# The start of a two-layer attention kernel: a block of its own for the first normalisation, and the sums of three weight matrices divided and queued anew

## The chip, the cores and the metric

The kernel runs on one core of a Trainium2 chip. The metric is the device time of one execution in microseconds (us), as the median of several runs; lower is better. Besides, one execution was taken by the hardware profiler, and all times of single instructions come from that one. The core has five engines that run side by side, each through its own list of instructions in order, and wait for each other through semaphores: TensorE (PE in the profile) multiplies matrices, VectorE (DVE) and ScalarE (ACT) work on tiles, GpSimd (POOL) works on tiles and issues transfers, SyncE (SP) issues transfers only.

## The reference

The input is a batch of 8 images of 32 x 32 positions with 512 channels, in float32. Two layers follow each other; each adds the result of an attention over the group-normalised input to the input:

```
x = x + conv0(_gn(x))     # softmax(q k^T * 32**-0.5) v, 16 heads of 32, then w_proj and b_proj
x = x + conv1(_gn(x))     # 4 heads of 128, with relative position logits from pos_emb_w and pos_emb_h, then Wo
_gn(v): mean and variance over the positions and the 16 channels of each of 32 groups, eps 1e-5
```

Here q, k and v are products of the normalised input (1024 positions x 512 channels per batch) with 512 x 512 weights, all in float32.

## The kernel before

**Tiles and stages.** One batch is a block of 128 partitions x 4 chunks x 1024 positions: the channels lie on the partitions, so x is kept transposed. There are eight such blocks of memory in one pool (`block`, line 75); they are handed out anew as soon as the last use of an old one is over, and then the first write of the new one waits for it. A loop over the batches weaves together the first attention of batch b, the second layer of batch b − 1 and the loading and first projections of batch b + 1.

**Seven products.** Each 512 x 512 projection is done with seven products of half-size matrices instead of eight. For that, each weight matrix needs four differences of its quarters (`add_up`, line 138), and each input four sums and differences of its quarters, the forms (`forming`, line 332; f_xn in the profile). `seven` (line 390) runs the products in the order 0, 5, 1, 4, 6, 2, 3 into three banks x, y and z, and copies or adds the results between them: p1 and p7 are copies by ScalarE (L399, L418), a and b are sums by VectorE (L404, L412), and the four quarters of the result are written by ScalarE (L475), VectorE (L478, L481) and GpSimd (L485). In the profile these banks carry the name of what is projected: x_v, y_v, z_v for v, and so on. The second product into y of a unit (number 4) starts over in y when a has been read out of it, and the third (number 2) when b has been.

**What stands at the start.** `load_first` (line 802) loads the first batch's rows (x_rows) through the queues of SP and ScalarE, then v's weights through SP. TensorE transposes the rows, ScalarE copies the result to x0T (L827), TensorE does six matmuls that nobody reads (L831), and VectorE gathers statistics (L251, L252). `put_away` (line 216) then writes x0T to DRAM through SP's queue (d in the profile), because it is added again after the attention; `group_norm` (line 257) makes mean and variance by some ten small operations on VectorE (L277 to L288), the reciprocal root on GpSimd (L292, rstd), and normalises x0T in place in four quarters (L296). The forms follow. GpSimd makes v's differences meanwhile (L147) and stores them to DRAM (L149). q's and k's weights are loaded by SP after that, and all eight of their differences are made by VectorE behind the last form (`issue_after(last_form[0].ins)`, which is an order, not a wait). Then `before_first` (line 838) runs the first unit of v, of q and of k, and the loop begins.

The second batch is fetched by `load` (line 780): pieces of x (xs, four transfers of 64 KB for each) through SP's queue into three buffers, transposed by VectorE (L794). A scheduler places the instructions of each engine in an order of its own; `issue_after` binds it. A transfer of SP also waits until one issued eight transfers earlier has landed.

Of the kernel before, what the change touches and what calls it, by code (L numbers as in the profile page):

```python
# [13 lines left out]
ALU = mybir.AluOpType  # L14
# [13 lines left out]
def quick_path(  # L28
# [23 lines left out]
    nc = tc.nc  # L52
# [22 lines left out]
    def block(name, shape=None, dtype=F32):  # L75
        return mem.tile(shape or [P, CC, N], dtype, tag="block", name=name, bufs=BLOCKS)

    def chunks(block):
        return [block[:, i, :] for i in range(CC)]
# [36 lines left out]
    check_at = [0]  # L116


    HC, HN = CC // 2, NB // 2

    def quarter(w, i):
# [3 lines left out]
    class Matrix:  # L125
# [9 lines left out]
            whole = t[:, : CC // 2, :].rearrange("p a (b n) -> p (a b) n", n=NB)  # L135
            queue.dma_start(whole, self.w)

        def add_up(self, engine, store, keep=False):

            t = self.t  # L140
            whole = t[:, : CC // 2, :].rearrange("p a (b n) -> p (a b) n", n=NB)
            sums = t[:, CC // 2 :, :].rearrange("p a (b c n) -> p (a b) c n", c=HC, n=HN)
            b11, b12, b21, b22 = [quarter(whole, i) for i in (11, 12, 21, 22)]
            for i, (x, y) in enumerate(
                [(b12, b11), (b22, sums[:, 0]), (b22, b12), (b21, sums[:, 1])]
            ):
                engine.tensor_tensor(sums[:, i], x, y, op=ALU.subtract)  # L147
            d = dram.tile([P, 4, HC, HN], F32, tag="sums", name=f"ws_{self.name}", bufs=8)
            store.dma_start(d, sums)  # L149
            self.t = d  # L150
            self.kept = (whole, sums) if keep else None
# [17 lines left out]
    class Stream:  # L169
# [41 lines left out]
        def ahead(self):  # L211
            use = next(self.uses, None)
            if use is not None:
                self.load(*use)

    def put_away(xT, name):
        kept = []
        for cc in range(CC):
            d = dram.tile([P, N], F32, tag="kept", name=f"d_{name}_{cc}", bufs=4 * CC)
            nc.sync.dma_start(d, xT[cc])  # L220
            kept.append(d)
        return kept

# [10 lines left out]
    def load_blocks(b, cc, h):  # L234

        xs = mem.tile([P, NB // 32, 32], F32, tag="row", name=f"xs_{b}_{cc}_{h}", bufs=3)
        for a in range(P // 32):
            nc.sync.dma_start(
                xs[32 * a : 32 * a + 32],
                by_blocks(xf[b, h * NB : (h + 1) * NB, :], cc * P + 32 * a),  # L240
            )
        return xs.rearrange("p t i -> p (t i)")
# [11 lines left out]
            s.rearrange("p h s -> p (h s)"),  # L254
        )

    def group_norm(st, xT, name, after=None, behind=None):

        mv = st.pop("mv")

        def averages(out, src, tag):
            total = small.tile([P, 2], F32, tag=f"total{tag}", name=f"total{tag}_{name}")
            nc.vector.tensor_reduce(
                total, src.rearrange("p (g k) -> p g k", k=GROUP_CHANNELS), axis=AX.X, op=ALU.add
            )
            nc.vector.tensor_scalar(
                out.rearrange("p (g k) -> p g k", k=GROUP_CHANNELS),
                total.unsqueeze(2).to_broadcast([P, 2, GROUP_CHANNELS]),
                1.0 / GROUP_CHANNELS,
                None,  # L270
                op0=ALU.mult,
            )

        turned = small.tile([P, 32], F32, tag="turned", name=f"turned_{name}")

        with tc.issue_after(after().ins) if after is not None else nullcontext():
            nc.vector.transpose(turned, mv)  # L277
        avg = small.tile([P, 2, 32], F32, tag="avg", name=f"avg_{name}")
        averages(avg[:, 0, :], turned, 0)

        nc.vector.tensor_sub(turned, turned, avg[:, 0, :])
        nc.vector.tensor_mul(turned, turned, turned)
        averages(avg[:, 1, :], turned, 1)
        back = small.tile([P, 2, 32], F32, tag="back", name=f"back_{name}")
        nc.vector.transpose(back.rearrange("p a c -> p (a c)"), avg.rearrange("p a c -> p (a c)"))
        mean = back[:, 0, :CC]
        var = small.tile([P, CC], F32, tag="var", name=f"var_{name}")
        nc.vector.scalar_tensor_tensor(  # L288
            var, back[:, 0, CC : 2 * CC], GN_EPS, back[:, 1, :CC], op0=ALU.add, op1=ALU.add
        )  # L290
        rstd = small.tile([P, CC], F32, tag="rstd", name=f"rstd_{name}")
        nc.gpsimd.tensor_tensor(rstd, var, neg_half, op=ALU.pow)  # L292
        yield 0
        for cc in range(CC):
            with tc.issue_after(behind().ins) if behind is not None else nullcontext():
                nc.vector.tensor_scalar(  # L296
                    xT[cc],
                    xT[cc],
                    mean[:, cc : cc + 1],
                    rstd[:, cc : cc + 1],  # L300
                    op0=ALU.subtract,
                    op1=ALU.mult,
                )
            if cc % 2:
                yield 0
# [3 lines left out]

    begun = [None]  # L310
    half_done = [None]
    last_form = [None]

    added = [None]

# [41 lines left out]
    def forms(x, name, room=None):  # L357
        got = []

        def whole():  # L360
            got.append((yield from forming(x, name, room)))

        run(whole())
        return got[0]
# [415 lines left out]
    def load(b, st):  # L780

        x = xT = None
        parts = [(cc, h) for cc in range(CC) for h in range(NH)]
        ahead = [load_blocks(b, *parts[i]) for i in range(2)]
        for i, (cc, h) in enumerate(parts):
            xs = ahead.pop(0)
            if i + 2 < len(parts):
                ahead.append(load_blocks(b, *parts[i + 2]))
            if h == 0:
                yield 0  # L790
            if x is None:
                x = block(f"x0T_{b}")
                xT = chunks(x)
            nc.vector.transpose(xT[cc][:, h * NB : (h + 1) * NB], xs)  # L794
            if h == NH - 1:
                statistics(st, xT, cc, f"0_{b}")
        yield 0
        st["kept"] = put_away(xT, f"0_{b}")
        yield from group_norm(st, xT, f"0_{b}")
        st["xn"] = yield from forming(x, f"xn0_{b}", behind=lambda: added[0])  # L800

    def load_first(st):

        rows = block("x_rows", [P, NT, C])
        for t in range(NT):
            queue = nc.scalar if t % 2 else nc.sync
            queue.dma_start(rows[:, t, :], xf[0, t * P : (t + 1) * P, :])
        WV0.fetch(nc.sync)
        x = block("x0T_0")
        xT = chunks(x)  # L810
        for h in range(NH):
            if h == 0:
                whole = psum.tile([P, CC, NB], F32, tag="ps", name="turned_0", bufs=1)
                banks = [whole[:, cc, :] for cc in range(CC)]
            else:
                banks = [bank(f"turned_1_{cc}") for cc in range(CC - 1)]
                banks.append(psum.tile([P, NB], F32, tag="acc", name="turned_1", bufs=1))
            for t in range(NT // NH):
                for cc in range(CC):
                    nc.tensor.transpose(  # L820
                        banks[cc][:, t * P : (t + 1) * P],
                        rows[:, h * (NT // NH) + t, cc * P : (cc + 1) * P],
                        ident,
                    )
            for cc in (0, 2, 1, 3):
                part = xT[cc][:, h * NB : (h + 1) * NB]
                nc.scalar.copy(part, banks[cc])  # L827

        idle = psum.tile([P, CC, NB], F32, tag="ps", name="idle", bufs=1)
        for t in range(6):  # L830
            nc.tensor.matmul(idle[:, t % CC, :], ident, rows[:, t, :], start=True, stop=True)  # L831
        for cc in (0, 2, 1, 3):
            statistics(st, xT, cc, "0_0")
        st["kept"] = put_away(xT, "0_0")
        run(group_norm(st, xT, "0_0"))
        st["xn"] = forms(x, "xn0_0")

    def before_first(st):

# [139 lines left out]
    def run(part):  # L979
        for _ in part:  # L980
            pass
# [34 lines left out]
    WQ0, WK0, WV0 = [Matrix(w_qkv, i * C, f"qkv{i}") for i in range(3)]  # L1016
# [19 lines left out]

    states = [{} for _ in range(B)]
    load_first(states[0])
    WV0.add_up(nc.gpsimd, nc.gpsimd, keep=True)
    for m in (WQ0, WK0):  # L1040
        m.fetch(nc.sync)

        with tc.issue_after(last_form[0].ins):
            m.add_up(nc.vector, nc.gpsimd, keep=True)
    fill_sel()
    stream = Stream(plan)

    def other_sums():
        for m in (WP, WQ1, WK1, WV1, WO):
            m.fetch(nc.gpsimd)  # L1050
            m.add_up(nc.gpsimd, nc.gpsimd)
            yield 0

    def at_once(do):
# [1 line left out]
        return  # L1056
        yield

    run(before_first(states[0]))
    for b in range(B + 1):  # L1060
        rest, total = [], 0
        s = [None] * 2 + states + [None] * 2
# [547 lines left out]
```

## Time and profile before

| | us |
|---|---|
| median of 3 runs (lowest, highest) | 3852.97 (3852.47, 3856.44) |
| profiled execution | 3854.03 |
| its span, first to last instruction | 3852.2 |
| mean granted TensorE clock | 0.997 |
| TensorE busy | 3793.3 |
| VectorE busy | 2555.5 |
| TensorE's wait ahead of the first v product | 5.4 |

Busy time is the time in which an engine had an instruction under way. A row of the order of time gives start, length, engine, line, operation and tiles, the count of equal instructions that were merged, and in brackets the idle time before it with what ended it. Matmuls overlap, so a row's length is a little more than its share of the engine. The granted clock is TensorE's, as a share of full speed.

### The profile page before, as it was taken

What the parts mean: (1) busy time and instruction counts of PE and PEld (TensorE: products, weight loads), DVE (VectorE), ACT (ScalarE), POOL (GpSimd) and SP (SyncE); (2) the same over time, 40 slices, a digit from 0 to 9 for tenths busy, and PEclk for the clock granted to TensorE, in tenths of its full rate; (3) what the DMA queues carried; (4) which work ended last, traced back from release to release, by engine and by line L of the source; (5) the groups of instructions that cost most, each with busy time, mean ns of one, the idle gap of its engine ahead of it and who ended that gap; (6) DMA issues with size and microseconds to landing.
All of it is one profiled execution on the core that took longest, in us unless ns stands there. A gap on an engine that the chain in (4) does not pass through costs nothing. (4 is left out here: it accounts for less than half of the span.)

```text
span 3852.2 us, 79876 instructions
## 1 busy us (share of the span) xinstructions
PE 3793.3 (98%) x34478; PEld 1376.7 (36%) x34478; DVE 2555.5 (66%) x2964; ACT 1760.4 (46%) x1830; POOL 620.8 (16%) x400
## 2 busy tenths in 40 slices
PE   8999999999999999999999999999999999999998
PEld 4222244232443224432344323433234332334353
DVE  6777675676755867568665686656866568665545
ACT  2554554545444454444544445444454445553132
POOL 2341101121101210112100121111210112001201
PEclk9999999999999999999999999999999999999999
DMA  6122120143202322023220231203411033110321
GB/s 184 60 87 79 42 60 3 37 126 65 59 6 73 98 57 56 12 89 85 49 55 16 93 91 37 52 20 96 91 39 43 24 97 77 31 39 31 105 45 26
DMA packets 482983, 234.72 MB, mean 61 GB/s; under 512 B 269600, under 2 KB 461376, under 8 KB 481600
## 3 DMA queue, kind: packets, MB, share of 16 engines
q1 hardware_dynamic: 470992, 213.74, 20.6%
q0 software_dynamic: 2608, 13.70, 1.0%
q8 instruction: 273, 4.47, 0.5%
q10 hardware_dynamic: 9024, 2.10, 0.3%
q14 instruction: 86, 0.70, 0.1%
HBM read 170.72 MB, written 58.72 MB: 60 GB/s over the span
## 5 line engine op out<-in xcount | busy, mean ns | idle before, releaser
L604 ACT ACTIVATE e<-ps 128x2048 f32<-128x2048 f32 x512 | 961.7, 1878 | 839.6 <-PE ps L596 633.5
L626 DVE TENSOR_TENSOR es<-es,e 128x2048 f32<-128x2048 f32 x384 | 893.3, 2326 | 405.9 <-ACT e L604 403.0
L596 PE MATMUL ps<-q,k 32*64 32x512 f32 x8192 | 578.3, 613 | 18.7 <-ACT e L604 18.7
L615 PE MATMUL acc<-e,v 128*32 128x512 f32 x4096 | 547.4, 606 | 0.0
L714 ACT ACTIVATE e<-ps 128x512 f32<-128x512 f32 x512 | 305.7, 597 | 506.9 <-PE ps L712 437.4
L711 PE MATMUL ps<-q,k 128*128 128x512 f32 x1024 | 525.0, 594 | 0.3 <-DVE posT L697 0.3
L723 PE MATMUL acc<-e,v 128*128 128x512 f32 x1024 | 522.0, 593 | 0.3 <-ACT e L714 0.3
L581 POOL TENSOR_TENSOR q<-q,su 128x512 f32<-128x512 f32 x128 | 210.4, 1644 | 1548.9 <-DVE su L577 1428.6
L734 DVE TENSOR_TENSOR es<-es,e 128x512 f32<-128x512 f32 x384 | 291.5, 759 | 249.8 <-ACT e L714 247.2
L712 PE MATMUL ps<-posT,sel 128*128 128x512 f32 x512 | 406.6, 794 | 0.0
L711 PEld LDWEIGHTS ps<-q,k 128*128 128x128 f32 x1024 | 192.5, 190 | 230.2 <-issue 218.5
L596 PEld LDWEIGHTS ps<-q,k 32*64 32x64 f32 x8192 | 120.5, 129 | 411.7 <-issue 221.7
L723 PEld LDWEIGHTS acc<-e,v 128*128 128x128 f32 x1024 | 193.1, 189 | 147.3 <-issue 92.8
L615 PEld LDWEIGHTS acc<-e,v 128*32 128x32 f32 x4096 | 81.3, 108 | 411.9 <-issue 363.8
L624 DVE TENSOR_TENSOR es<-e,e 128x2048 f32<-128x2048 f32 x64 | 173.0, 2704 | 32.4 <-ACT e L604 32.4
L561 DVE STREAM_TRANSPOSE tu<-su 128x512 f32<-128x512 f32 x128 | 90.5, 707 | 97.0 <-ACT su L559 95.4
L712 PEld LDWEIGHTS ps<-posT,sel 128*128 128x128 f32 x512 | 97.3, 190 | 122.5 <-issue 122.5
L559 ACT COPY su<-sums 128x512 f32<-128x512 f32 x128 | 74.9, 585 | 130.3 <-PE sums L636 80.3
L697 DVE TENSOR_TENSOR posT<-pp,posT 32x512 fp32r<-32x512 f32 x128 | 111.9, 875 | 32.0 <-ACT posT L692 30.7
L485 POOL TENSOR_TENSOR k<-b_k,p_k 128x512 f32<-128x512 f32 x32 | 51.4, 1606 | 485.3 <-ACT p_k L418 485.3
L692 ACT CAST posT<-pp 32x512 fp32r<-32x512 f32 x128 | 105.9, 827 | 46.4 <-PE pp L679 45.2
L485 POOL TENSOR_TENSOR v<-b_v,p_v 128x512 f32<-128x512 f32 x32 | 51.6, 1614 | 440.0 <-ACT p_v L418 431.9
(209 smaller groups left out, 4550.1 us busy)
## 6 DMA issues: line engine op xcount, KB each, us to landing
w_qkv<-ws_qkv SPq DMA_DIRECT2D x168, 128.0 KB, 2.5
d<-x0T SPq DMA_DIRECT2D x32, 512.0 KB, 3.2
x1T<-d SPq DMA_DIRECT2D x32, 512.0 KB, 6.0
d<-x1T SPq DMA_DIRECT2D x32, 512.0 KB, 3.6
x2T<-d SPq DMA_DIRECT2D x32, 512.0 KB, 6.4
w_qkv<-in_L_conv_w_qkv SPq DMA_DIRECT2D x126, 128.0 KB, 2.2
out<-ot SPq DMA_DIRECT2D x240, 64.0 KB, 2.0
xs<-in_x SPq DMA_DIRECT2D x224, 64.0 KB, 2.6
```

What stands on the lines that cost most here:

```text
L581: nc.gpsimd.tensor_tensor(dst, dst, su, op=ALU.mult)
L596: nc.tensor.matmul(ps[some, r, :], k[m][rows, j * P + 64 * i : j * P + 64 * i + 64], q[m][rows, h * NB : (h + 1) * NB], start=True, stop=True,
L604: nc.scalar.activation(e, ps, AF.Exp, scale=D0 ** -0.5)
L615: nc.tensor.matmul(acc[r * D0 : (r + 1) * D0, :], v[:, j, c0 : c0 + D0], e[:, r, :], start=(j == blocks[0]), stop=(j == blocks[-1]),)
L624: nc.vector.tensor_add(state["esum"], state["first"], e)
L626: nc.vector.tensor_add(state["esum"], state["esum"], e)
L697: nc.vector.tensor_sub(rest, logits, greater)
L711: nc.tensor.matmul(ps, k[h][:, keys], q[:, h, queries], start=True, stop=False)
L712: nc.tensor.matmul(ps, sel_flat[:, keys], posT[:, h, queries], start=False, stop=True)
L714: nc.scalar.activation(e, ps, AF.Exp, scale=1.0 / math.sqrt(D1))
L723: nc.tensor.matmul(acc, v[:, j, h * D1 : (h + 1) * D1], e, start=(j == 0), stop=(j == NT - 1),)
L734: added[0] = nc.vector.tensor_add(state["esum"], state["esum"], e)
```

## The change

1. The first batch is normalised into a new block xn0_0 (`group_norm` gets `out`); the forms are made from that. x0T is only read from then on.
2. The loads of q's and k's weights are issued right behind v's, in `load_first`.
3. The first pieces of the second batch are placed behind the last transfer of a put-away (`put`), for batch 1 alone.
4. `add_up` takes an engine for each of its four differences. v's first two stay with GpSimd and its last two go to VectorE; q's stay with VectorE. Each that is VectorE's is placed behind the last form.
5. k's differences are woven into `before_first` from its fourth step on, instead of standing ahead of it.

```diff
+    last_form = [None]
...
-        def add_up(self, engine, store, keep=False):
+        def add_up(self, engines, store, keep=False):
...
-                engine.tensor_tensor(sums[:, i], x, y, op=ALU.subtract)
+
+                engine = engines[i]
+                with tc.issue_after(last_form[0].ins) if engine is nc.vector else nullcontext():
+                    engine.tensor_tensor(sums[:, i], x, y, op=ALU.subtract)
...
+    put = [None]
...
-            nc.sync.dma_start(d, xT[cc])
+            put[0] = nc.sync.dma_start(d, xT[cc])
...
-    def group_norm(st, xT, name, after=None, behind=None):
+    def group_norm(st, xT, name, after=None, behind=None, out=None):
...
-                    xT[cc],
+                    xT[cc] if out is None else out[cc],
...
-        ahead = [load_blocks(b, *parts[i]) for i in range(2)]
+
+        with tc.issue_after(put[0].ins) if b == 1 else nullcontext():
+            ahead = [load_blocks(b, *parts[i]) for i in range(2)]
...
-        WV0.fetch(nc.sync)
+        for m in (WV0, WQ0, WK0):
+            m.fetch(nc.sync)
...
-        run(group_norm(st, xT, "0_0"))
-        st["xn"] = forms(x, "xn0_0")
+
+        xn = block("xn0_0")
+        run(group_norm(st, xT, "0_0", out=chunks(xn)))
+        st["xn"] = forms(xn, "xn0_0")
...
-    WV0.add_up(nc.gpsimd, nc.gpsimd, keep=True)
-    for m in (WQ0, WK0):
-        m.fetch(nc.sync)
-
-        with tc.issue_after(last_form[0].ins):
-            m.add_up(nc.vector, nc.gpsimd, keep=True)
+    WV0.add_up([nc.gpsimd] * 2 + [nc.vector] * 2, nc.gpsimd, keep=True)
+    WQ0.add_up([nc.vector] * 4, nc.gpsimd, keep=True)
     fill_sel()
     stream = Stream(plan)
+
+    def key_sums():
+        WK0.add_up([nc.vector] * 4, nc.gpsimd, keep=True)
+        yield 0
...
-            m.add_up(nc.gpsimd, nc.gpsimd)
+            m.add_up([nc.gpsimd] * 4, nc.gpsimd)
...
-    run(before_first(states[0]))
+    run(woven(before_first(states[0]), key_sums(), 3, 1))
```

More of the change, by code (lines that the diff above doesn't have):

```diff
@@ L311, in quick_path @@
     half_done = [None]
-    last_form = [None]
     added = [None]
```

## The prediction

> **What bounds the kernel now.** I read the page's busy shares first, then TensorE's waits in the first 200 us, then the start engine by engine in order of time. TensorE is the bound nearly everywhere:
>
> ```profile
> PE 3793.3 (98%) x34478; PEld 1376.7 (36%) x34478; DVE 2555.5 (66%) x2964; ACT 1760.4 (46%) x1830; POOL 620.8 (16%) x400
> ```
>
> So a change pays only where TensorE waits or runs at a low clock. Comparing the two programs engine by engine, every order is the same from the first batch's q projection on, apart from names and one moved load of weights. Only the first 40 us or so can change by themselves. There TensorE's largest wait is the one between the idle matmuls of L831 and the first product with v's weights:
>
> ```profile
> PE x_v L320 <- issue: 5.4, 1, 5.4
> PE x_v L320 <- DVE x0T L296: 0.7, 1, 0.7
> PE x_v L320 <- ACT p_v L399: 0.7, 1, 0.7
> PE y_v L320 <- DVE a_v L404: 0.4, 1, 0.4
> ```
>
> (Engine, line, what released it, us in total, times, longest.) What happens ahead of it, in order of time (start, us, engine, line, idle before and its releaser):
>
> ```profile
> 16.44 1.26 POOL L147 TENSOR_TENSOR prep_qkv<-prep_qkv 128x512 f32<-128x512 f32 x1
> 16.49 1.25 DVE L281 TENSOR_TENSOR turned<-turned,avg 128x32 f32<-128x32 f32 x1
> 17.78 0.19 DVE L282 TENSOR_TENSOR turned<-turned 128x32 f32<-128x32 f32 x1
> ...
> 18.97 1.04 POOL L292 TENSOR_TENSOR rstd<-var,neg_half 128x4 f32<-128x4 f32 x1 [0.28 <-DVE var L288]
> 20.54 0.81 DVE L296 TENSOR_SCALAR x0T<-x0T,back,rstd 128x1024 f32<-128x1024 f32 x1 [1.66 <-DMA d<-x0T]
> 21.66 0.81 DVE L296 TENSOR_SCALAR x0T<-x0T,back,rstd 128x1024 f32<-128x1024 f32 x1 [0.31 <-DMA d<-x0T]
> 23.22 0.81 DVE L296 TENSOR_SCALAR x0T<-x0T,back,rstd 128x1024 f32<-128x1024 f32 x1 [0.74 <-DMA d<-x0T]
> 26.96 0.81 DVE L296 TENSOR_SCALAR x0T<-x0T,back,rstd 128x1024 f32<-128x1024 f32 x1 [2.93 <-DMA d<-x0T]
> 27.81 1.23 DVE L353 TENSOR_TENSOR f_xn<-x0T 128x1024 f32<-128x1024 f32 x1
> ...
> 32.48 4.90 DVE L147 TENSOR_TENSOR prep_qkv<-prep_qkv 128x512 f32<-128x512 f32 x8
> 37.30 0.68 DVE L404 TENSOR_TENSOR a_v<-y_v,p_v 128x512 f32<-128x512 f32 x1
> ```
>
> Each quarter of the normalisation overwrites a piece of x0T that is still on its way to DRAM, and waits for that transfer. The statistics are also held up: L281 takes 1.25 us where L282, of the same size, takes 0.19, exactly as long as POOL's last difference of v's weights. And while TensorE idles its clock falls (columns: window, length, then PE, PEld, DVE, ACT and POOL busy, granted clock, DMA share, GB/s):
>
> ```profile
> 20.00:21.00 1.00, 0.00 (x0) 0.00 (x0) 0.46 (x1) 0.00 (x0) 0.01 (x1) 0.61 1.04 426
> ...
> 30.00:31.00 1.00, 1.00 (x20) 0.47 (x16) 1.00 (x2) 0.32 (x1) 0.00 (x0) 0.77 0.53 125
> ```
>
> Between the two every window shows 0.50. A mean of 0.61 puts the drop at 20.22, one of 0.77 the return at 30.46.
>
> **What the skill says.** "TensorE: Matmul & The Clock Gate", Part 1: the clock halves after an idle window of about 3.4 us, returns after a busy one, and the windows run freely. The trace agrees on the size: 30.46 − 20.22 = 10.24 us, three windows of 3.41. It is harsher than "idle": further on, a wait of only 1.85 us (to 380.78) also brings the half clock. "SBUF — State Buffer", section "SBUF: two separate sides": VectorE's two-input operations and GpSimd's take one shared port pair by an exclusive lock; L281 shows it. "DMA: Bandwidth & Descriptors", section "Queues, rings and completion order": an engine consumes a queue's descriptors in ring order. So q's and k's weights, queued behind v's, should not delay v's; POOL's start at 12.63, on v's arrival, should stay.
>
> **The change, part by part.** All times are from the span's start.
>
> *Two of v's four differences leave POOL.* POOL's remaining two end at 12.63 + 2 × 1.24 = 15.1, before the small operations of L277 to L288. L281 falls from 1.25 to 0.19 and L266 from 0.46 to 0.18: 1.3 us off, variance at 17.5, rstd 17.6 to 18.65. If v's weights came a little later the conflict would stay; so this step is worth 0 to 1.3. I take 1.3.
>
> *The normalisation writes a block of its own.* The four waits for the transfer go. Four quarters of 0.81 from 18.7 end at 22.0, against 27.77: 5.8 earlier, of which 1.3 is the step above. The forms (27.81 to 32.48, 4.67 us) then end at 26.7. The block is paid by reuse: k takes the block of the raw rows, long free, and the second batch's x0T takes that of the first, whose transfer must have landed by about 53 us. Before, all this traffic was through by 31.5. No cost.
>
> *Sums on VectorE.* Two more of 0.61 go ahead of q's: 1.2 us. But the order changes too: five sums, then a_v (L404), four sums, b_v (L412), one sum, where before all eight stood ahead of a_v. So a_v is done at 26.7 + 5 × 0.61 + 0.69 = 30.5 and b_v, at the earliest, at 30.5 + 4 × 0.61 + 0.69 = 33.6.
>
> *SP's queue.* The loads of q's and k's weights move ahead of the second batch's pieces, one 128 KB load of weights moves ahead of the put-away, and three transfers of pieces move from ahead of it to behind. All twelve transfers of the first three pieces stand behind SP's put-away; their first reader is the transpose at 57.22. No cost. POOL's stores of the sums follow VectorE: v's leaves at 28 instead of 17.99, q's at about 31 instead of 35.88, k's after 34 instead of 37.68. SP waits for q's store (13.1 us now) with the weights and later pieces queued behind; it ends earlier than before.
>
> *TensorE through this.* My mark is the point where all seven v products, eight matmuls of x_q and one of y_q are issued: 42.51 now (y_v restarts at 40.79 and takes 1.72). A product takes 1.72 warm and 3.44 cold.
> Bound by VectorE alone: y_v restarts at 33.7 after b_v; + 1.72, + 0.75 for seven z_v matmuls, + 1.72 for eight of q = 37.9. Gain 4.6.
> With the clock as it now falls, at 20.2: TensorE idles from 16.10 to 19.6, long enough for a drop. Four x_v matmuls, a wait for the second quarter until 20.45, twelve cold (2.6) and the tail to 23.3, the copy of p1 to 24.0, thirteen cold (2.8) to 26.8. The window from 23.63 to 27.05 is then some 90% busy, against 77% in the one that brought the clock back before; so the clock returns at 27.05. The rest of y_v and x_v to 29.0, z_v to 30.7, one x_q, wait for the copy of p7 to 31.6, one z_v, y_v 31.7 to 33.4, eight z_v to 34.3, b_v to 34.4, y_v to 36.2, seven z_v 36.9, eight of q 38.65. Gain 3.9.
> If the clock returns only at 30.46, the same walk puts y_v's first product at 30.4 and ends at 40.6. Gain 1.9.
> I take 3.8. From the mark to 69 us TensorE has no gap, and later waits hang on the same instructions, so the shift is carried to the end. Against the profiled execution (3854.03, span 3852.2) that is 3850.2; it stands 1.06 above the median of the three runs, 3852.97, so the forecast is 3849.2. It is 0.10%: inside the 0.2% (7.7 us) that a measurement of this kernel can tell from no change.
>
> **Rivals.** *The clock eats it:* it stays at half until 30.46 or v's weights land late enough to keep the lock at L281. Gain 0.6 (1.9 less 1.3) to 1.9: 3851 to 3852.4. For it: windows 64% and 79% busy did not bring the clock back before. Against: the new windows are fuller. 0.2.
> *More than the start:* three later waits (to 146.10, 331.03 and 380.78) now end in a half-clock window of 3.41 us, 1.7 us lost each. The windows run freely, so a shifted start may spare some. Two spared gives 3.8 + 3.4 = 7.2, 3845.8; all three 8.9, 3844.1. Against: the execution at hand has no reason to be unlucky. 0.13.
> *Slower:* the same lottery the other way. About ten waits of 1.2 to 1.9 us (to 243.47, 273.41, 304.00, 865.53 and so on) now pass at full clock; each new drop costs up to 1.7. From three new drops on (5.1 against 3.8) the kernel is slower than before: 3854.3; it takes seven to pass 0.2%. The slowest run shown, 3856.44, may be such a one. 0.09.
> *The change does not free VectorE:* a late piece at the transpose of 57.22, behind which b_k waits, or a hidden wait of the normalisation. The programs show only POOL's rstd ahead of the latter, and the former has over 20 us to spare: 0.02, price 0 to 4, 3849 to 3853.
>
> **How the numbers follow.** The forecast case, gain 2.5 to 5.5, has 0.56. Its own range is 3847.5 to 3850.5. To leave out no more than 2 in 10, I reach to two spared drops below and to one lost gain with one new drop above: 3845.5 to 3853.8. Faster by over 0.2% needs all three drops spared or a start better than VectorE's bound: 0.06. Slower by over 0.2% needs seven drops or something unseen: 0.03. Within: 0.91.
>
> **What would show it.** Right: the statistics' subtraction (L281) at 0.2 us; the normalisation's four quarters back to back from about 18.7 with no wait for the put-away; forms from 22.0; a_v near 30, b_v near 34; y_v's last product starting near 34.4 instead of 40.79; the transpose of the second batch near 53.4. A clock back at full by about 27. Wrong: v's weights landing after 13.5 us, a clock at half beyond 28, the transpose at 57 waiting for a DMA, or a different count of half-clock windows between 140 and 390 us.

## The result and the profile after

| | before | after |
|---|---|---|
| median, us (lowest, highest; 17 runs each) | 3853.90 (3852.22, 3856.44) | 3847.82 (3846.09, 3850.03) |
| profiled execution, its span | 3854.03, 3852.2 | 3848.35, 3846.6 |
| TensorE's wait ahead of the first v product | 5.4 | 3.5 |
| L281 before, L289 after (statistics) | 1.25 | 0.19 |
| last quarter of the normalisation ends | 27.77 | 21.81 |
| first b of q starts (L412, L419) | 48.00 | 43.06 |

The ratio is 0.9984, with a 95% interval of 0.9978 to 0.9991: 6.1 us, or 0.16%, and by the interval 3.5 to 8.5 us. The forecast was 3849.2. By the bound of 0.2% this is no change, and yet the whole interval lies on the faster side.

TensorE's waits in the first 200 us of the changed kernel (engine, line, what released it, us in total, times, longest):

```profile
PE x_v L327 <- issue: 3.5, 1, 3.5
...
PE x_v L327 <- ACT p_v L406: 0.7, 1, 0.7
```

Of the four waits at the start that were shown of before, two are left: 5.4 became 3.5, 0.7 for the copy of p_v is as it was, and those for a quarter of x0T and for a_v are gone. The changed kernel in order of time (start, us, engine, line, what, and in brackets the idle time before with its releaser):

```profile
13.84 1.27 POOL L152 TENSOR_TENSOR prep_qkv<-prep_qkv 128x512 f32<-128x512 f32 x1
16.33 0.19 DVE L289 TENSOR_TENSOR turned<-turned,avg 128x32 f32<-128x32 f32 x1
17.75 1.04 POOL L300 TENSOR_TENSOR rstd<-var,neg_half 128x4 f32<-128x4 f32 x1 [1.70 <-DVE var L296]
18.83 2.98 DVE L304 TENSOR_SCALAR xn<-x0T,back,rstd 128x1024 f32<-128x1024 f32 x4 [1.16 <-POOL rstd L300]
...
26.52 3.09 DVE L152 TENSOR_TENSOR prep_qkv<-prep_qkv 128x512 f32<-128x512 f32 x5
29.53 0.68 DVE L411 TENSOR_TENSOR a_v<-y_v,p_v 128x512 f32<-128x512 f32 x1
30.13 2.48 DVE L152 TENSOR_TENSOR prep_qkv<-prep_qkv 128x512 f32<-128x512 f32 x4
32.53 0.68 DVE L419 TENSOR_TENSOR b_v<-y_v,p_v 128x512 f32<-128x512 f32 x1
```

The quarters are back to back and wait only for rstd. GpSimd's second difference is over at 15.1, so the statistics meet nothing. It had started at 12.49 (the first one, 12.63 before), so v's weights were not held up by those queued behind them. a_v stands between five sums and four, b_v ahead of the last.

From the first b of q on, every matched TensorE instruction is 4.94 us earlier, up to 139 us. Then the shift varies with the half-clock windows of each execution, between 2.9 and 6.6 us earlier, and is 6.0 at the last matched instructions (the spans differ by 5.6). The experiments therefore compare two things: the time, and the **mark**, which is from here on the start of the first b of q.

### The profile page after: what moved, and what is told of

The parts are those of the page before. It is cut to its first block, busy times and chain, and to the rows that moved or that the text cites. A ratio compares the mean times of both kernels' runs of the same rounds, so it can differ in the third digit from the quotient of the medians.

```text
span 3846.6 us, 79883 instructions
## 1 busy us (share of the span) xinstructions
PE 3789.4 (99%) x34478; PEld 1376.3 (36%) x34478; DVE 2555.1 (66%) x2966; ACT 1760.2 (46%) x1830; POOL 621.6 (16%) x398
## 4 chain that ended last, share of the span: by engine, by line
PE 88%; DVE 7%; ACT 2%; issue 2%; DMA 0%; SPq 0%; POOL 0%; DVEq 0%; ACTq 0%; POOLq 0%
PE ps L603 12%; PE ps L718 11%; PE acc L730 11%; PE acc L622 11%; PE y_q L327 4%; PE y_v L327 4%; PE y_k L327 4%; PE ps L719 3%; PE x_q L327 3%; PE x_v L327 3%; PE z_k L327 3%; PE x_k L327 3%; PE z_q L327 3%; PE z_v L327 3%; DVE es L633 2%; ACT e L611 2%
```

## The experiments

The line numbers in the diffs' text and in the rows are each kernel's own. The kernel before was timed beside each: 3853.78, 3853.39, 3853.43 and 3853.64 us. This is what came of all of them, from the latest mark to the earliest:

| kernel | mark | time, us | ratio (95%) |
|---|---|---|---|
| before with 12 idle matmuls | 51.74 | 3856.16 | 1.0008 (1.0001–1.0014) |
| before, second profile | 48.02 | 3853.37 | 1.0001 (0.9992–1.0010) |
| v's halves alone | 46.80 | 3853.14 | 1.0000 (0.9991–1.0008) |
| v's store late | 45.74 | 3851.19 | 0.9994 (0.9985–1.0002) |
| all but the block | 45.35 | 3850.49 | 0.9993 (0.9984–1.0002) |
| all but the halves | 43.95 | 3847.90 | 0.9985 (0.9978–0.9992) |
| block alone | 43.84 | 3849.14 | 0.9987 (0.9980–0.9994) |
| k's sums not woven | 43.63 | 3848.63 | 0.9988 (0.9981–0.9995) |
| after, second profile | 42.94 | 3847.72 | 0.9985 (0.9978–0.9991) |
| q's and k's sums late, 10 idle matmuls | 42.34 | 3848.38 | 0.9986 (0.9979–0.9993) |
| q's and k's sums late | 42.32 | 3847.70 | 0.9985 (0.9978–0.9991) |

An interval is 2.5 to 3.5 us wide to either side. By the time, the kernels with the block are faster than the kernel before, but they can't be told from each other, and the three with marks from 46.80 to 45.35 can't be told from the kernel before. What a part brings is therefore read from the mark, which differs by 0.02 and 0.12 between two profiles of one program.

### Which part of the change brings the gain

**The block alone**, put into the kernel before:

```diff
-                    xT[cc],
+                    xT[cc] if out is None else out[cc],
...
-        run(group_norm(st, xT, "0_0"))
-        st["xn"] = forms(x, "xn0_0")
+        xn = block("xn0_0")
+        run(group_norm(st, xT, "0_0", out=chunks(xn)))
+        st["xn"] = forms(xn, "xn0_0")
```

> The kernel before with the own block for the first normalisation alone; sums, queues and weaving as before. Mark: the start of b_q (L412 for q), 48.00 us before and 43.06 after, a shift of 4.94. Theory (the waits for the put-away are the gain): GpSimd still makes all four of v's differences, so L281 stays at 1.25 us and rstd ends at 20.0; the four quarters follow without a wait and end near 23.0, forms near 27.7; a shift of 4.0 to 4.3 at the mark, 0.7 short of the full change. Rival (the division of the sums and the weaving carry it): a shift of under 2. Whole time 3849 to 3850.

VectorE in order of time, block alone:

```profile
29.39 0.68 DVE L404 TENSOR_TENSOR a_v<-y_v,p_v 128x512 f32<-128x512 f32 x1
29.99 3.40 DVE L147 TENSOR_TENSOR prep_qkv<-prep_qkv 128x512 f32<-128x512 f32 x5
33.31 0.68 DVE L412 TENSOR_TENSOR b_v<-y_v,p_v 128x512 f32<-128x512 f32 x1
```

The mark moves by 4.16 of the 4.94, as expected, and the time is 4.6 us below the kernel before. The statistics still meet GpSimd's last difference (L281 stays at 1.25), so the quarters begin at 19.89, 1.06 later than in the changed kernel. The scheduler has put a_v and b_v between the sums although nothing is woven here.

**All but the halves**: the changed kernel, with v's four differences all on GpSimd.

```diff
-    WV0.add_up([nc.gpsimd] * 2 + [nc.vector] * 2, nc.gpsimd, keep=True)
+    WV0.add_up([nc.gpsimd] * 4, nc.gpsimd, keep=True)
```

> The changed kernel with all four of v's differences on GpSimd again. Theory: L281 is held up again (1.25 us), rstd ends near 20.0 instead of 18.8, but two sums of 0.61 less stand ahead of a_v: the mark (b_q) lies 0 to 0.8 later than 43.06; whole time 3847.5 to 3849. Equal to the own block alone, if the queues and the weaving are worth nothing. Rival (the division is worth its 1.3 us of lock in full): 44.3.

The mark is 0.89 later than in the first profile of the changed kernel and 1.01 later than in the second, a little more than expected. L289 is at 1.25 again and the quarters start at 19.93. So the halves are worth 0.9 to 1.0 on top of the block: the 1.1 us that the statistics gain, less what the two sums cost on VectorE, where they turn out to be nearly covered. Against the block alone the mark differs by 0.11: the order of the loads, the pieces behind the put-away and the weaving together bring nothing here. The time, 3847.90, shows nothing of the halves' part.

**K's sums not woven**: in the changed kernel, k's differences stand ahead of the first projections.

```diff
+    WK0.add_up([nc.vector] * 4, nc.gpsimd, keep=True)
...
-    run(woven(before_first(states[0]), key_sums(), 3, 1))
+    run(before_first(states[0]))
```

> The changed kernel, with k's four differences made ahead of the first projections instead of woven into them. If the scheduler places a_v and b_v between the sums by itself, as it did where only the block was changed, the first b of q stays at 43.0 to 43.5 us (43.06 in the changed kernel) and the time is the changed kernel's, 3847 to 3849. Rival, the weaving brings a part of the gain: all eight sums of q and k stand ahead of b_v, which then comes 1.2 to 2.5 us later, with the first b of q at 44.3 to 45.6, and the time is 3849 to 3851.

VectorE in order of time, not woven:

```profile
19.08 2.98 DVE L304 TENSOR_SCALAR xn<-x0T,back,rstd 128x1024 f32<-128x1024 f32 x4 [1.16 <-POOL rstd L300]
...
26.77 6.10 DVE L152 TENSOR_TENSOR prep_qkv<-prep_qkv 128x512 f32<-128x512 f32 x10
32.79 0.68 DVE L411 TENSOR_TENSOR a_v<-y_v,p_v 128x512 f32<-128x512 f32 x1
...
35.67 0.69 DVE L419 TENSOR_TENSOR b_v<-y_v,p_v 128x512 f32<-128x512 f32 x1 [1.37 <-PE y_v L327]
```

Neither expectation fits as it was put. All ten sums do stand ahead of a_v, and b_v comes 3.1 later than in the changed kernel, as the rival had it or worse; yet the mark is only 0.57 later, 43.63, and 0.25 of that is there at the quarters already (19.08 against 18.83). The order of TensorE changed with the sums: it does z_v and x_q matmuls where y_v would have waited. So weaving is worth some 0.3 us at the mark, not much more than two profiles of one program differ by, and a_v and b_v are not as hard a bound as the prediction's walk made them.

### Why the versions in place came out better than expected

Two experiments leave the normalisation in place. **v's halves alone**, put into the kernel before:

```diff
-    WV0.add_up(nc.gpsimd, nc.gpsimd, keep=True)
+    WV0.add_up([nc.gpsimd] * 2 + [nc.vector] * 2, nc.gpsimd, keep=True)
```

> The kernel before with v's last two differences on VectorE alone; the normalisation stays in place. Theory: L281 falls to 0.2 us and rstd ends near 18.7, but the quarters wait for the put-away as before, the last until 26.9; two more sums of 0.61 stand ahead of a_v. The mark (b_q) shifts by 0 to 1.2 us to later; whole time 3853 to 3855. Rival (the shared lock is the gain): 1.3 us earlier.

**All but the block**, the changed kernel normalising x0T in place:

```diff
-        run(group_norm(st, xT, "0_0", out=chunks(xn)))
-        st["xn"] = forms(xn, "xn0_0")
+        run(group_norm(st, xT, "0_0"))
+        st["xn"] = forms(x, "xn0_0")
```

> The changed kernel with the normalisation in place again; everything else of the change kept. Theory: the quarters wait for the put-away until about 26.5 to 27; the mark (b_q) falls back to 47.5 to 49, so nothing of the 4.94 is left; whole time 3852 to 3855. Rival (sums, queues and weaving carry the gain): the mark stays below 46.

Both theories missed: the halves alone moved the mark 1.2 us earlier, not later, and all but the block gave 2.65, where nothing was to be left. The rivals' numbers came (1.3 earlier, and a mark below 46), but the lock is not the cause of the first: with the halves alone the first quarter starts no earlier than before (20.54), since it waits for the put-away. The first and the last quarter with the halves alone, then the issue of the put-away and the last quarter with all but the block (in order of time):

```profile
20.73 0.81 DVE L300 TENSOR_SCALAR x0T<-x0T,back,rstd 128x1024 f32<-128x1024 f32 x1 [3.33 <-DMA d<-x0T]
...
24.50 0.81 DVE L300 TENSOR_SCALAR x0T<-x0T,back,rstd 128x1024 f32<-128x1024 f32 x1 [0.58 <-DMA d<-x0T]
```

```profile
11.10 2.27 SPq L228 DMA_DIRECT2D d<-x0T  x4
...
23.28 0.81 DVE L304 TENSOR_SCALAR x0T<-x0T,back,rstd 128x1024 f32<-128x1024 f32 x1 [0.56 <-DMA d<-x0T]
```

They still wait for the put-away in each quarter, but the last one starts 2.5 and 3.7 us sooner than before (26.96). The mark gains 1.0 to 1.3 us less than that, about what v's two sums take on VectorE ahead of a_v (1.2). Two reasons were possible: the landing differs from execution to execution, or something that both edits moved had been in its way. A second profile of the kernel before, unchanged, answers the first:

> The kernel before once more, for a second profile of the same program. Put-away theory: the landing of the first batch's put-away differs from one execution to the next, because nothing but the traffic of the moment decides it; then the fourth quarter of the normalisation starts anywhere from 24 to 27 us (26.96 in the first profile), and b_v and the first b of q (48.00 there) move with it by up to 2.5 us. Rival: the order of SP's queue decides it and the landing is the same in each execution: fourth quarter within 0.3 us of 26.96, b of q within 0.3 of 48.00, and the earlier landings of the two in-place experiments come from their changed queue. On the later stalls: if half-clock windows behind them are a lottery, the list of windows after 140 us (146.51, 330.83 and 382.03 in the first profile) differs; if they belong to the program, it is the same.

The fourth quarter starts at 26.99 and the mark is 48.02: the landing belongs to the program. What both edits moved is GpSimd's store of v's differences, 1 MB, which must wait for VectorE's sums. So it was **moved alone**, in the kernel before, behind the stores of q's and k's:

```diff
-    WV0.add_up(nc.gpsimd, nc.gpsimd, keep=True)
+    WV0.add_up(nc.gpsimd, None, keep=True)
...
+    with tc.issue_after(WQ0.stored.ins):
+        nc.gpsimd.dma_start(*WV0.unstored)
```

> The kernel before, with one thing moved: GpSimd's store of v's differences (1 MB, at 17.99 us) stands behind its stores of q's and k's. If this store shares the DMA engines with the put-away and so delays its last quarter, the normalisation's fourth quarter starts at about 24.5 us instead of 26.96 to 26.99 (24.50 where v's halves were divided and the store was late by itself), and a_v and the first b of q follow: 45.6 us instead of 48.00, time 3851 to 3852. Rival, the put-away waits for the queue of SyncE and the second batch's pieces ahead of it: the fourth quarter stays at 27.0, b of q at 48.0, and the time is that of the kernel before.

The last quarter, and the store, in order of time:

```profile
24.70 0.81 DVE L299 TENSOR_SCALAR x0T<-x0T,back,rstd 128x1024 f32<-128x1024 f32 x1 [0.57 <-DMA d<-x0T]
...
35.97 0.53 POOL L1049 DMA_DIRECT2D ws_qkv<-prep_qkv  x1
```

The fourth quarter waits 0.57 instead of 2.93, the mark is 45.74 and the time 3851.19: a move of one store brings 2.3 us at the mark, close to half of what the whole change brings there. (The time is 2.2 us lower, with an interval that includes no change.) The store, issued at 17.99 by GpSimd, was in the way of a transfer that SyncE had issued at 12.22. That is what the Trainium skill says ("DMA: Bandwidth & Descriptors", section "Issuing engines are not separate DMA queues"): transfers of all engines run on the same 16 DMA engines and interleave. The last quarter starts another 1.2 us sooner with all but the block than with the halves alone. That fits the put-away's own place, issued at 11.10 there, 1.1 earlier than before; this was not tested alone.

### What the clock costs at the start

**The kernel before with twelve idle matmuls** instead of six (L831):

```diff
-        for t in range(6):
-            nc.tensor.matmul(idle[:, t % CC, :], ident, rows[:, t, :], start=True, stop=True)
+        for t in range(12):
+            nc.tensor.matmul(idle[:, t % CC, :], ident, rows[:, t % NT, :], start=True, stop=True)
```

> The kernel before with twelve matmuls that nobody reads instead of six, so that TensorE is busy until about 21.4 us and then has only a short wait for the first normalised quarter: its clock should stay full, or fall later, at the start. If VectorE sets the pace there (a_v and b_v behind eight sums), a full clock brings at most 0.4 us at the first b of q (48.00) and the time stays within 0.5 of 3853.8. Rival, the half clock of 20.22 to 30.46 costs part of the 5 us: the first b of q comes 2 to 5 us earlier and the time is 3849 to 3852.

Both theories missed. Two windows of this kernel (window, length, PE, PEld, DVE, ACT and POOL busy, granted clock, DMA share, GB/s):

```profile
28.00:29.00 1.00, 0.98 (x10) 0.29 (x10) 1.00 (x1) 0.00 (x0) 0.00 (x0) 0.91 0.75 116
...
35.00:36.00 1.00, 1.00 (x19) 0.51 (x12) 1.00 (x3) 0.11 (x1) 0.04 (x1) 0.68 0.00 0
```

The clock is full until 28.82 and then falls for 6.83 us, two windows. That is shorter than before (20.22 to 30.46), and TensorE is busy in 5.28 us of it, against 7.58 of the low 10.24 before, so less work ran at half clock. But the scheduler also orders the products anew around the extra matmuls. The first y_v product now stands ahead of x_v's last ones, and TensorE waits for its form, as it does not before:

```profile
30.53 3.64 PE L320 MATMUL y_v<-prep_qkv,f_xn 128*32 128x256 f32 x32 [1.55 <-DVE f_xn L353]
```

a_v comes at 37.39, as before (37.30), but b_v slips to 42.92, the mark to 51.74, and the kernel is 2.8 us slower. What of it is the order and what the place of the half clock was not separated. Idle work kept TensorE's clock up for 8.6 us longer and brought nothing.

**The changed kernel, second profile:**

> The changed kernel once more, for a second profile. Nothing of its start waits for the put-away, so the first b of q should be within 0.3 us of 43.06, with v's weights landing where they did and L289 at 0.19 us. The half clock at the start should be one or two windows of 3.41 us, and those after 140 us (166.87 and 327.30 in the first profile) differ if they are a lottery and stay if they belong to the program.

One window of the changed kernel, in its first and then in its second profile:

```profile
20.00:21.00 1.00, 1.00 (x16) 0.35 (x12) 1.00 (x2) 0.00 (x0) 0.00 (x0) 0.55 1.04 426
```

```profile
20.00:21.00 1.00, 0.96 (x24) 0.44 (x20) 1.00 (x3) 0.00 (x0) 0.00 (x0) 1.00 1.01 414
```

One execution runs at half clock from 20.10 to 23.51, the other not at all, though the program is the same. Their marks are 43.06 and 42.94, and all 0.12 between them is there at the first quarter already (18.83, 18.71). So in the changed kernel this half-clock window at the start costs nothing: the products wait for VectorE again behind it.

### Is there more to gain at the start

**q's and k's sums late**: in the changed kernel, q's four differences stand behind a_v, k's behind b_v.

```diff
-    WQ0.add_up([nc.vector] * 4, nc.gpsimd, keep=True)
+    WQ0.promise()
+    WK0.promise()
...
+    def late_sums():
+        WQ0.make_sums(nc.gpsimd, begun[0])
+        yield 0
+        WK0.make_sums(nc.gpsimd, half_done[0])
...
-    run(woven(before_first(states[0]), key_sums(), 3, 1))
+    run(woven(before_first(states[0]), late_sums(), 1, 2))
```

(`promise` sets up the tiles; `make_sums` is the loop of `add_up` with each difference placed behind the instruction that is given, and the store.)

> The changed kernel, with q's four differences placed behind a_v and k's behind b_v, so that VectorE makes only v's two between the forms and a_v. If VectorE still sets the pace at the start, a_v and b_v come 1.2 us or more earlier and the first b of q stands at 41.9 us instead of 43.06 and 42.94; the time is about 1.2 us below the changed kernel's, 3846 to 3847. Rival, TensorE or ScalarE's copies already set the pace, or q's differences are then late for its second product: the first b of q stays at 42.9 to 43.5 and the time at 3847.8.

a_v comes at 27.80 and b_v at 30.93, 1.7 and 1.6 earlier than in the changed kernel, but the mark only 0.6 to 0.7 (42.32), between the two expectations, and the time is the changed kernel's. The same with **ten idle matmuls** instead of six:

> The kernel with q's and k's differences placed late, and with ten matmuls that nobody reads instead of six ahead of v's products, so that TensorE has hardly a wait ahead of the first product at 19.7 us. If TensorE and its one half-clock window (20.26 to 23.67) set the pace now that VectorE's sums are out of the way, no window of half clock appears before 140 us and the first b of q comes 0.4 to 1.0 us earlier than 42.32, at 41.3 to 41.9. Rival, VectorE or ScalarE's copies still set it: 42.2 to 42.4; a second rival, the half clock only falls later, as in the kernel before with twelve such matmuls: 43 or later. The time follows by as much, 3847.0, 3847.7 or above 3848.4, which can't be told from the changed kernel's 3847.8.

No half clock is left before 139 us, and the mark is 42.34. TensorE's order of time shows why:

```profile
22.78 0.63 PE L344 MATMUL x_v<-prep_qkv,xn 128*32 128x256 f32 x6 [0.70 <-ACT p_v L423]
24.63 1.93 PE L344 MATMUL y_v<-prep_qkv,f_xn 128*32 128x256 f32 x32 [1.22 <-DVE f_xn L377]
```

What the full clock gains is waited away again, at 24.63 for a form. The first rival holds, and neither version beats the changed kernel by more than can be measured.

### Where the last microsecond comes from

The second profiles make a clean pair: both have a half-clock window of 3.41 us behind the same two waits (146.04 and 330.36 before, 140.86 and 325.18 after). The kernel after is 5.08 us earlier from the mark on, 5.02 to 5.14 up to 300 us, then at once 6.26 at 304, and 5.5 at the end. The step at 304 in order of time, first before and then after (second profiles):

```profile
295.54 0.58 ACT L559 COPY su<-sums 128x512 f32<-128x512 f32 x1 [1.95 <-PE sums L636]
...
298.22 1.27 POOL L581 TENSOR_TENSOR q<-q,su 128x512 f32<-128x512 f32 x1 [21.23 <-DVE su L577]
298.46 3.17 DVE L624 TENSOR_TENSOR es<-e,e 128x2048 f32<-128x2048 f32 x1 [0.39 <-ACT e L604]
...
302.01 1.88 ACT L604 ACTIVATE e<-ps 128x2048 f32<-128x2048 f32 x1 [3.58 <-PE z_v L320]
...
303.94 1.12 PE L596 MATMUL ps<-q,k 32*64 32x512 f32 x16 [1.87 <-ACT e L604]
```

```profile
290.73 0.58 ACT L566 COPY su<-sums 128x512 f32<-128x512 f32 x1 [2.23 <-PE sums L643]
...
293.37 2.29 DVE L631 TENSOR_TENSOR es<-e,e 128x2048 f32<-128x2048 f32 x1
293.41 3.39 POOL L588 TENSOR_TENSOR q<-q,su 128x512 f32<-128x512 f32 x1 [21.53 <-ACT e L611]
...
295.75 1.88 ACT L611 ACTIVATE e<-ps 128x2048 f32<-128x2048 f32 x1 [2.42 <-DVE es L631]
...
297.68 1.12 PE L603 MATMUL ps<-q,k 32*64 32x512 f32 x16 [0.63 <-ACT e L611]
```

Two operations with two inputs each meet. Before, GpSimd starts 0.24 ahead of VectorE, and VectorE's takes 3.17 instead of 2.29; the exponent behind it (ScalarE, e) and TensorE wait. After, VectorE starts 0.04 ahead and it is GpSimd's that takes 3.39 instead of 1.27, and nothing waits for it. The Trainium skill ("SBUF — State Buffer", section "SBUF: two separate sides") says that whichever of the two starts first has the port pair for the whole instruction; the durations agree. That is 0.88 us of the step. Another 0.29 lies ahead of the exponent: before, it starts 0.38 us after VectorE's operation has ended (301.63), after only 0.09 (295.66). The turn of order comes from ScalarE's copy, which starts 1.19 us after the first of its matmuls before and 1.48 after.

All profiles divide alike: TensorE's wait here is 1.9 in the six profiles of kernels that normalise in place (before twice, twelve idle matmuls, halves, late store, all but the block) and 0.6 in the seven of kernels that have the block.

The traces show how the block gets here. With it, ScalarE's first write to k's block (at 53 us) has four more waits ahead of it, in all seven profiles and in none of the six, so whatever follows stands four places further down in ScalarE's list. And in all 13 profiles the 192nd recorded instruction of that list, waits counted, starts 0.32 to 0.33 us after the wait just ahead of it, where 0.04 is usual. In the kernels without the block the 192nd is the exponent; with it, it is the copy, and the exponent, now the 196th, starts after 0.04. So the 0.28 us that the exponent loses before is lost by the copy after; that is the copy's lateness, and it turns the order of VectorE and GpSimd. The same delay shows a multiple of 128 places further on where nothing else holds the instruction (the 1088th, 2112th and 2752nd of the kernel before). Why these places are slow is open, and no kernel with four more waits but without the block was run. Nothing in the idea of the change aims at this: that 1.2 us came with the block is luck.

## Why the prediction came out

The forecast was 3849.2 and the median is 3847.82, inside the likeliest case's own range of times. The gain of 6.1 us, however, is above that case's 2.5 to 5.5; that the time fell inside is in part luck with the sample of the kernel before, as the last but one point says. By its steps:

- **v's halves leave POOL, 1.3 us off the statistics.** The mechanism is right (L281 1.25, L289 0.19; 1.25 again when the halves are undone). The size is 1.06 to 1.10 at the first quarter, and 0.9 to 1.0 at the mark.
- **Four quarters of 0.81 from 18.7 to 22.0.** 18.83 to 21.81: back to back, four take 2.98, not 3.24. Forms end at 26.5 instead of 26.7.
- **Sums: a_v done at 30.5, b_v at 33.6.** 30.2 and 33.2. The order was read rightly, five and four, but the weaving that makes it is worth only some 0.3 us at the mark.
- **SP's queue and POOL's stores: no cost.** True for the changed kernel; no wait for a transfer appears. What the step did not see is that the same moves have a price where the normalisation stays in place: v's store alone was 2.3 us of the wait that the block takes away. The expectations of the two experiments in place failed for that reason.
- **TensorE through this: gain 3.8, of a bound of 4.6 by VectorE and 3.9 with a clock low until 27.05.** This is the term that was mis-sized. The gain at the mark is 4.94 and 5.08. The clock was low for one window, until 23.51, or for none, and it made no difference; so the 0.7 to 0.8 taken off for it was nothing. The rest is b_v, 0.4 earlier than worked out. The argument that a fuller window brings the clock back doesn't come out of the lines of before either: TensorE was busy for 2.71 of 3.41 us in the second low window, after which the clock stayed low, and for 2.69 in the third (79%, not 77%), after which it returned.
- **"The shift is carried to the end."** It is, but for one step: the wait to 304.00, which the prediction counted among those that now pass at full clock, fell from 1.9 to 0.6, in each profile with the block. That is 1.2 us which no step held; the comparison of the two programs found the same orders and did not see ScalarE's four waits. With it the sum is 4.94 + 1.2 = 6.1, the difference of the two medians; but in the clean pair only 5.5 of 6.26 is left at the end, and the medians' difference has an interval of 3.5 to 8.5, so that the two agree to the tenth is chance.
- **The median.** 1.06 was taken off for the profiled execution standing above the median of three. Against the larger sample, 3853.90, it stands only 0.1 above; this hid nearly 1 us of the two sizes above. Two gains too small and a starting point too low stood against each other.
- **Rivals.** The clock did not eat the gain. Half-clock windows come and go from execution to execution: after 140 us (end left out) they are three and two in the two profiles of the kernel before, two and two in those of the changed one. In the second profiles, where they agree in place, the gain is still 5.5, more than the start was held to bring. So "more than the start" holds, though by the wait at 304 and not by spared windows. No new drop made it slower. The change did free VectorE; the second batch's transpose came at 52.52.

## What to carry to other kernels

An in-place write behind a transfer was held up here by a store of another queue: before a new buffer is bought, look for a large store that nobody awaits in that stretch, since moving it alone brought 2.3 us at the mark, against 4.2 for the block. A change at the start can add waits to another engine's list, and a few places further down in that list decided, 240 us later, who came first at a shared port; so compare the lists with their waits, and check each later wait that ends within some tenths of a microsecond of another. Idle matmuls to hold the clock brought nothing here: once they came with a worse order of the products, once the gain was waited away at the next input.

## What the runs showed of the hardware

- The half clock comes in lengths of 3.41 us or twice or three times that (10.24, 6.83, 3.41; the stretch at the very end left out), and the same program has it at the start in one execution and not in another. The Trainium skill ("TensorE: Matmul & The Clock Gate", Part 1) says that the windows are free-running and the ramp is run-variable; the two profiles of the changed kernel agree (3.41 us at 20.10, none). How busy a window must be to bring the clock back these runs don't show.
- Which of two engines starts first at the shared port pair, by 0.24 or by 0.04 us, decided 0.9 us of TensorE's time, and it came out the same way in each profile of a program.
- ScalarE's 192nd recorded instruction starts some 0.28 us later than others after a wait (0.32 to 0.33 against 0.04), whatever instruction it is, in all 13 profiles.
- Four equal VectorE operations took 0.81 us each when each waited for a transfer and 2.98 together back to back.
